# Repeating 1/sum by ScalarE and four transposes, with a new model of transfers and new leads in a list-scheduled Mamba and local-attention kernel

## The chip, the cores and the metric

The kernel runs on one core of a Trainium2 chip. The metric is the device time of one execution in microseconds; lower is better. A core has these engines, each with its own queue of instructions, worked off in order: PE (TensorE, matmuls; its weight loads are shown as PEld), DVE (VectorE), ACT (ScalarE), POOL (GpSimd) and SP (SyncE, which here issues nearly all transfers). Engines wait for each other by semaphores.

## The reference

The input is x, 4096 tokens of 256 features in float32. The output is x, plus a Mamba block, plus a two-layer local transformer, both applied to the same normalized x:

```
xn = layernorm(x)
out = x + mamba(xn) + local_transformer(xn)
```

The Mamba block projects 256 features to 2 x 512, convolves the first half over 4 tokens, and runs a recurrence over the tokens with 512 channels of 16 states each; the result is gated and projected back to 256. The transformer has two layers, each with local attention and an MLP of 682 gated hidden units. Attention has 8 heads of 64 features and windows of 128 tokens; a query sees the keys of its own window and of the window before:

```
attn = softmax(where(mask, -big, q @ k.T))   # per head and window
o = attn @ v                                 # 8 heads x 64 = 512 features
x = x + o @ wo
```

Softmax divides by the sum of the exponentials, one number for each query and head. The kernel multiplies the unnormalized `attn @ v` by 1/sum afterwards.

## The kernel before

**Tiles and stages.** The 4096 tokens are 16 stages of 256 tokens; each layer of the transformer goes through all 16, so there are 32 steps (l, s). A step projects two windows of 128 tokens (project), attends for both (attend), projects out (project_out) and runs the MLP (mlp). Beside them the Mamba block runs in 8 blocks of 512 tokens, each with 4 groups of 128 channels; one group of one block takes about one step. For each group, recur goes over the 16 states in 8 pairs: two loads of bc, copied to all partitions (L742 on, issued by SP at L451), a product u on POOL (L748), for each state a decay on ACT (L757), a scan on DVE (L762) and a product on DVE (L772), and transposes on PE that add up y (L784).

**Attention, around the change.** attend takes the heads in two groups of four. For each group PE multiplies queries and keys (L972), DVE masks and takes the largest (L987), ACT takes the exponential and its sum over the keys into den (L997), PE turns the probabilities (L1010), ACT copies them (L1014), and PE multiplies with V (L1026) into the bank po. There the features of a head lie over 64 partitions and the queries over columns. After both groups, den holds the sums with queries over partitions. DVE takes the reciprocal (L1043). To multiply, 1/sum has to lie like po: spread (L1049) has PE multiply one column of den, read 64 times as weights, by the identity, for each of 8 heads, in two halves of the array (part "columns"). ACT copies po into OT (L1055), DVE multiplies OT by the spread bank pd (L1056), and project_out reads OT (L1067).

**What sets the order.** Nothing in the code is in its final order. Each function records pieces of work by add (engine, estimated us, instructions, tiles read and written). A piece has a key: the time, in steps, at which its stage is due, minus its lead `soon`. Plan.order then simulates the engines: whenever one is free it takes, among the pieces whose inputs are ready and whose buffers are free, the one with the smallest key. Pieces with keys beyond the first open one plus AHEAD are not looked at. The instructions are emitted in the order of the simulated starts, and each engine on the chip then works off its own list in order. The estimates and the leads are therefore only an order: they are no waits. On PE a change of `part` (rows, columns, or the full array) is booked with SWITCH and avoided where another piece is nearly as urgent. `late` is the time from the end of an issue to the landing of a transfer. `holds` says which buffers a piece takes before it writes them. Buffers near the change: 5 PSUM banks, 2 OT tiles, 3 bc tiles, 3 u tiles, 2 PSUM tiles of decays.

**The planner's price of a transfer** is one line, in which kb is written out by hand at each call:

```
add("SP", 0.1, ..., late=2.4 + kb / 150.0, soon=soon)
```

The weights of each layer are loaded by load_qkv and load_rest; load_rest also has PE work out the shift of the MLP's bias (L487) and DVE scale w1 (L503).

Of the kernel before, what the change touches and what calls it, by code (L numbers as in the profile page):

```python
# [27 lines left out]
P = 128  # L28
# [3 lines left out]
TB = 512  # L32
# [10 lines left out]
AHEAD = 2.960000  # L43
# [93 lines left out]
class Plan:  # L137
# [4 lines left out]

    def __init__(self):
        self.works = []
        self.key = 0.0
# [35 lines left out]
    def order(self):  # L181
# [4 lines left out]
        part = ""  # L186
# [16 lines left out]
        while len(done) < len(self.works):  # L203
# [74 lines left out]
            w.start, w.end = start, start + w.us + self.TAIL[e] + w.late  # L278
# [35 lines left out]
def mamba_and_local_transformer(  # L314
# [38 lines left out]
    squares = buffer("sq", 2, [P, 512])  # L353
    turns = buffer("turn", 5, [P, HEADS, 2, DH // 2])
# [94 lines left out]
    def dma(kb, to, of, reads=(), writes=(), soon=0.0):  # L449

        add("SP", 0.1, lambda: nc.sync.dma_start(to(), of()), reads, writes, late=2.4 + kb / 150.0, soon=soon)  # L451

    def load_qkv(l):
        for s in range(3):
            cut = slice(s * INNER, (s + 1) * INNER)
            dma(
                512, lambda cut=cut: wqkv.ap[:, :, cut],
                lambda cut=cut: wqkv_d[l][:, cut].rearrange("(k p) n -> p k n", p=P), writes=[(wqkv, s)], soon=-0.25,
            )

    def load_rest(l):
        dma(512, lambda: wo.ap, lambda: wo_d[l].rearrange("(h p) n -> p h n", p=P), writes=[wo], soon=-0.09)
        for half in range(2):
            for m, n in ((0, WHOLE), (NM - 1, LAST)):
                to, of = w1_at(half, m), half * HID + m * MC
                dma(
                    n, lambda to=to, n=n: w1.ap[:, :, to : to + n],
                    lambda of=of, n=n: w1_d[l][:, of : of + n].rearrange("(k p) n -> p k n", p=P),
                    writes=[(w1, (half, m))], soon=-0.18,
                )  # L470
        whole = WHOLE
        dma(
            570, lambda: w2.ap[:, 0 : NM - 1, :],
            lambda: w2_d[l][0:whole, :].rearrange("(m p) n -> p m n", p=MC), writes=[(w2, 0)], soon=0.54,
        )
        dma(112, lambda: w2.ap[0 : HID - whole, NM - 1, :], lambda: w2_d[l][whole:HID, :], writes=[(w2, 1)], soon=-0.26)
# [28 lines left out]
        add("PE", 5.3, shift, [w1], [pb], soon=-0.73)  # L505
        add("DVE", 0.4, bias, [pb], [b1, b1x], soon=-0.28)
        add("DVE", 3.2, scale, [], [w1], port=True, soon=-0.24)
# [14 lines left out]
    def base_of(s):  # L522

        base = plan.value(rows_b)
        if s in sums:
            dma(256, lambda: base.ap, lambda: sums[s].ap, [sums[s]], [base], soon=-0.84)
            return base
        dma(256, lambda: base.ap, lambda: rows(x, s), writes=[base], soon=-0.12)
# [3 lines left out]
            ), [], [base], soon=-0.65,  # L532
# [3 lines left out]
    def finish(s, po, base):  # L536

        add("DVE", 0.6, lambda: nc.vector.tensor_tensor(base.ap, halves(po), base.ap, ALU.add), [po], [base], soon=-0.42)  # L538
        if s in sums:
            dma(256, lambda: rows(out, s), lambda: base.ap, [base], soon=0.37)  # L540
            return
        sums[s] = plan.fixed(dram.tile([P, NW, D], F32, tag=f"sum{s}", name=f"sum{s}"))
        dma(256, lambda: sums[s].ap, lambda: base.ap, [base], [sums[s]], soon=0.0)
# [4 lines left out]
    def shift_column(l, s):  # L548
        now = xts[l, s]
        if s == 0:  # L550
            add("POOL", 0.14, lambda: nc.gpsimd.memset(now.ap[:, 1, 0:1], 0.0), [], [(now, 0)], soon=0.49)
        else:
# [3 lines left out]
                [(old, 1)], [(now, 0)], soon=1.36,  # L556
            )

    def normalize(s):

        xb, mv, rstd, pt = (plan.value(b) for b in (rows_b, small["mv"], small["rstd"], banks))
        dma(256, lambda: xb.ap, lambda: rows(x, s), writes=[xb], soon=-0.18)
# [26 lines left out]
        add("DVE", 1.1, stats, [xb], [mv], soon=-1.39)  # L589
        add("ACT", 0.5, root, [mv], [rstd], soon=-0.35)  # L590
        add("DVE", 0.6, centre, [mv, rstd], [xb], port=True, soon=-0.91)
        now = xts[0, s] = plan.value(tokens)
        add("PE", 0.44, turn, [xb], [pt], holds=[now], soon=0.0)
        add("ACT", 0.48, lambda: nc.scalar.copy(now.ap[:, :, 1:], halves(pt)), [pt], [(now, 1)], soon=0.13)
        shift_column(0, s)
        dma(256, lambda: xn_d[s].ap, lambda: now.ap[:, :, 1:], [(now, 1)], [xn_d[s]], soon=-0.71)
# [3 lines left out]
    def reload(s):  # L600
        now = xts[1, s] = plan.value(tokens)
        dma(256, lambda: now.ap[:, :, 1:], lambda: x1_d[s].ap, [x1_d[s]], [(now, 1)], soon=-1.45)
# [6 lines left out]
    def in_half(i):  # L609
# [3 lines left out]
            lambda: in_wT[:, i * DI : (i + 1) * DI].rearrange("(k p) n -> p k n", p=P), writes=[w], soon=0.07,  # L613
# [3 lines left out]
    def in_proj(b, w, c, to):  # L617
# [9 lines left out]
        add("PE", 1.72, emit, [w, xms[b]], [pm], holds=[to], soon=0.09)  # L627
        return pm

    def front_load(b):  # L630
        xm = xms[b] = plan.value(xms_b)
        for i in range(PB):
            s = b * PB + i
            dma(
                256, lambda i=i: xm.ap[:, :, i * TS : (i + 1) * TS], lambda s=s: xn_d[s].ap, [xn_d[s]], [(xm, i)], soon=0.28
# [5 lines left out]
    def front_conv(b, c, w):  # L641
        xin, xc, tail = plan.value(rows_m), xcs[b], tails[b]
        edge = slice(c * (TAPS - 1), (c + 1) * (TAPS - 1))
        if b == 0:
            add("POOL", 0.14, lambda: nc.gpsimd.memset(xin.ap[:, 0 : TAPS - 1], 0.0), [], [(xin, 0)], soon=-0.34)
        else:
# [3 lines left out]
                [(old, c)], [(xin, 0)], soon=-0.31,  # L650
            )
        pm = in_proj(b, w, c, xin)
        add("ACT", 0.48, lambda: nc.scalar.copy(xin.ap[:, TAPS - 1 :], pm.ap), [pm], [(xin, 1)], soon=-0.44)
        if b < NB - 1:
            add(
                "POOL", 0.14, lambda: nc.gpsimd.tensor_copy(tail.ap[:, edge], xin.ap[:, TB:]), [(xin, 1)], [(tail, c)], soon=-0.19
            )
# [4 lines left out]
            ), [], [pm], soon=1.5,  # L662
# [8 lines left out]
        for j in range(TAPS - 1):  # L671
            add("DVE", 0.7, lambda j=j: tap(j), [xin, pm], [(xc, c) if j == TAPS - 2 else pm], soon=-0.95)

    def silu(v):
# [4 lines left out]
        add("ACT", 4.52, emit, [], [v], soon=-0.61)  # L679

    def front_dbl(b):
# [7 lines left out]
        add("PE", 3.43, emit, [xc], [px], holds=[xd], soon=-0.69)  # L689
        add("ACT", 0.48, lambda: nc.scalar.copy(xd.ap, px.ap[0:n]), [px], [xd], soon=-0.79)  # L690
        xds[b] = xd
        bc = bcs[b] = plan.fixed(dram.tile([2 * NS, TB], F32, tag=f"bc{b}", name=f"bc{b}"))
        dma(64, lambda: bc.ap, lambda: xd.ap[DTR:, :], [xd], [bc], soon=-0.28)

    def gate_conv(b, c, w):
# [4 lines left out]
        add("ACT", 0.48, lambda: nc.scalar.copy(sz.ap[:, c, :], pz.ap), [pz], [(sz, c)], soon=-1.39)  # L700

    def prepare(b, c):
# [7 lines left out]
            ), [xd], [pd], holds=[dt, e], soon=0.11,  # L710
# [3 lines left out]
        add("ACT", 0.59, lambda: nc.scalar.activation(e.ap[:, n], pd.ap, AF.Abs, bias=col("dt_b", c)), [pd], [e], soon=-0.35)  # L714
        add("ACT", 0.6, lambda: nc.scalar.activation(dt.ap, pd.ap, AF.Relu, bias=col("dt_b", c)), [pd], [dt], soon=1.17)
        add("ACT", 0.54, lambda: nc.scalar.activation(e.ap[:, n], e.ap[:, n], AF.Exp, scale=-1.0), [], [e], soon=-0.02)
        add(
            "DVE", 0.36, lambda: nc.vector.tensor_scalar(r.ap[:, n], e.ap[:, n], 1.0, -1.0, ALU.add, ALU.add),
            [e], [r], port=True, soon=0.7,
        )  # L720
        add("POOL", 1.22, lambda: nc.gpsimd.tensor_tensor(r.ap[:, n], e.ap[:, n], r.ap[:, n], ALU.subtract), [e], [r], soon=0.72)
        add("ACT", 0.6, lambda: nc.scalar.activation(e.ap[:, n], e.ap[:, n], AF.Ln, bias=one_t), [], [e], soon=-0.38)
        add("POOL", 1.22, lambda: nc.gpsimd.tensor_tensor(dt.ap, dt.ap, r.ap[:, n], ALU.add), [r], [dt], soon=1.1)
        add("POOL", 1.22, lambda: nc.gpsimd.tensor_tensor(dt.ap, dt.ap, e.ap[:, n], ALU.add), [e], [dt], soon=-0.41)
        add(
            "DVE", 0.61, lambda: nc.vector.tensor_tensor(dtx.ap, dt.ap, xc.ap[:, c, :], ALU.mult),
            [dt, (xc, c)], [dtx], port=True, soon=1.04,
# [3 lines left out]
    def recur(b, c, g):  # L731
# [6 lines left out]
        for s in range(2):  # L738
            w = plan.value(spreads)
            dma(  # L740
                256, lambda w=w: w.ap.rearrange("p n t -> p (n t)"),
                lambda s=s: bc.ap.rearrange("(s n) t -> s n t", s=2)[s, g * NG : (g + 1) * NG, :]  # L742
                .rearrange("n t -> (n t)").partition_broadcast(P), [bc], [w], soon=-0.15,
# [6 lines left out]
            ), [dtx, spread[0]], [u], soon=1.13,  # L750
        )
        for i in range(NG):
# [6 lines left out]
                ), [dt], [h], soon=0.32,  # L759
# [4 lines left out]
                ), [(u, i), (state, (c, n))], [h], soon=-0.6,  # L764
            )
            if b < NB - 1:
                add(
                    "ACT", 0.1, lambda h=h, n=n: nc.scalar.copy(state.ap[:, c, n : n + 1], h.ap[:, TB - 1 : TB]),  # L768
                    [h], [(state, (c, n))], alone=[h], soon=1.5,
# [4 lines left out]
                ), [h, spread[1]], [(u, i)], alone=[h], soon=-0.09,  # L774
# [4 lines left out]
        if n_sums == 1:  # L779
            add("POOL", 1.22, lambda: nc.gpsimd.tensor_tensor(u.ap[:, 0, :], u.ap[:, 0, :], u.ap[:, 1, :], ALU.add), [], [u], soon=-0.01)  # L780
# [13 lines left out]
        for i in range(n_sums):  # L794
            add("PE", 0.44, lambda i=i: collect(i), [(u, i)], [y], soon=0.31)

    def close(b, c):
# [3 lines left out]
        add("ACT", 0.48, lambda: nc.scalar.copy(ytv(), y.ap), [y], [yt], soon=0.43)  # L801

        def turn():
# [3 lines left out]
        add("PE", 0.44, turn, [yt], [py], soon=-0.05)  # L807
# [3 lines left out]
            ), [py], [(xc, c)], soon=1.5,  # L811
# [3 lines left out]
            [sz], [(xc, c)], soon=0.29,  # L815
        )

    def out_load():
# [3 lines left out]
            writes=[w], soon=0.29,  # L822
# [3 lines left out]
    def out_proj(b, i, w):  # L826
# [12 lines left out]
        add("PE", 3.44, emit, [w, xc, base], [po], soon=-0.75)  # L839
# [5 lines left out]
    def rotation(l, s):  # L845
        rot, trig = plan.value(rots), plan.value(trigs)
        dma(
            128, lambda: rot.ap, lambda: rot_d[s * TS : (s + 1) * TS].rearrange("(t p) s d -> p t s d", p=P),
            writes=[rot], soon=-0.22,
        )  # L850
        for i, scales in enumerate((qks, qkw)):
            for q in range(2):
# [6 lines left out]
                    ), [rot], [(trig, (i, q))], soon=-0.33,  # L859
# [3 lines left out]
    def project(l, s, t):  # L863
# [3 lines left out]
        def matmuls(q, holds):  # L867
# [10 lines left out]
            add("PE", 1.72, emit, [xb, (wqkv, q)], [pm], holds=holds, soon=-0.07)  # L878
# [4 lines left out]
        def norm(q, pm, sq):  # L883
            add("ACT", 0.48, lambda: nc.scalar.activation(sq.ap, pm.ap, AF.Square), [pm], [sq], alone=[pm], soon=-0.06)
# [3 lines left out]
                ), [sq], [(nrm, q)], soon=-0.52,  # L888
# [10 lines left out]
        def turned(parts, to):  # L899
            add("POOL", 1.22, lambda: nc.gpsimd.tensor_tensor(parts[0].ap, parts[0].ap, parts[1].ap, ALU.add), [parts[1]], [parts[0]], soon=-0.42)  # L900
# [9 lines left out]
            add("PE", 0.44, emit, [parts[0]], [pt], holds=[to], soon=-0.39)  # L910
# [456 lines left out]
```

## Time and profile before

| what | value |
|---|---|
| median of 3 runs | 1978.17 us (1977.82 to 1978.35) |
| the profiled execution's own time | 1979.39 us |
| its span in the profile | 1977.6 us |
| PE busy, instructions | 1917.6 us (97%), 13200 |
| DVE busy, instructions | 1742.4 us (88%), 3182 |
| ACT busy, instructions | 1490.5 us (75%), 3530 |
| POOL busy, instructions | 1411.3 us (71%), 1178 |
| mean clock granted to PE | 0.995 |
| DMA | 334.74 MB, mean 169 GB/s |

The span goes from the first to the last instruction of the core; the execution's own time is 1.8 us longer, which lies around the span. A float32 matmul has two records in the profile, a transpose one. Busy time is the time in which at least one record of an engine runs. A group is named by its line, its engine and what it writes and reads (out<-in); behind the bar stand its busy time, the mean of one record and the idle time of the engine just before it, with what ended that idle time. The chain that ended last is followed back from the last instruction.

### The profile page before, as it was taken

What the parts mean: (1) busy time and instruction counts of PE and PEld (TensorE: products, weight loads), DVE (VectorE), ACT (ScalarE), POOL (GpSimd) and SP (SyncE); (2) the same over time, 40 slices, a digit from 0 to 9 for tenths busy, and PEclk for the clock granted to TensorE, in tenths of its full rate; (3) what the DMA queues carried; (4) which work ended last, traced back from release to release, by engine and by line L of the source; (5) the groups of instructions that cost most, each with busy time, mean ns of one, the idle gap of its engine ahead of it and who ended that gap; (6) DMA issues with size and microseconds to landing.
All of it is one profiled execution on the core that took longest, in us unless ns stands there. A gap on an engine that the chain in (4) does not pass through costs nothing.

```text
span 1977.6 us, 37023 instructions
## 1 busy us (share of the span) xinstructions
PE 1917.6 (97%) x13200; PEld 1462.7 (74%) x13200; DVE 1742.4 (88%) x3182; ACT 1490.5 (75%) x3530; POOL 1411.3 (71%) x1178
## 2 busy tenths in 40 slices
PE   6999999999999999999999999999999999999997
PEld 3576777777777767777767777778777877777785
DVE  3789999999889999898997989889998898998895
ACT  2878877878777877777886787787887878777662
POOL 2668777777777777767785768877678767777773
PEclk9999999999999999999998999999999999999999
DMA  5445455644455445555465544455445654445453
GB/s 171 138 142 163 168 188 168 206 147 168 157 190 184 167 150 168 168 198 183 164 212 174 195 133 164 167 190 197 147 167 171 197 177 155 165 158 181 139 181 113
DMA packets 133928, 334.74 MB, mean 169 GB/s; under 512 B 13452, under 2 KB 57184, under 8 KB 133744
## 3 DMA queue, kind: packets, MB, share of 16 engines
q1 hardware_dynamic: 132752, 331.92, 50.7%
q8 instruction: 104, 1.70, 0.3%
q10 hardware_dynamic: 992, 0.46, 0.1%
q14 instruction: 80, 0.66, 0.1%
HBM read 315.03 MB, written 17.30 MB: 168 GB/s over the span
## 4 chain that ended last, share of the span: by engine, by line
PE 73%; DVE 12%; ACT 6%; DMA 4%; POOL 3%; issue 2%; SPq 0%; POOLq 0%; DVEq 0%; ACTq 0%
PE mm L873 12%; PE mm L1131 12%; PE y L784 7%; PE mm L1026 5%; PE mm L1067 5%; PE mm L972 5%; PE mm L623 5%; PE mm L1010 4%; PE mm L1213 4%; DVE da L762 3%; PE mm L1194 3%; DMA bc<-bc 2%; PE mm L905 2%; PE mm L1049 2%; DVE u L772 2%
## 5 line engine op out<-in xcount | busy, mean ns | idle before, releaser
L748 POOL TENSOR_TENSOR u<-dtx,bc 128x1024 f32<-128x1024 f32 x256 | 605.8, 2367 | 222.3 <-DMA bc<-bc 129.1
L762 DVE TENSOR_TENSOR_SCAN da<-da,state,u 128x512 f32<-128x512 f32 x448 | 562.2, 1278 | 60.7 <-POOL u L748 41.1
L757 ACT ACTIVATE da<-dt,negA 128x512 f32<-128x512 f32 x512 | 346.7, 693 | 95.6 <-DVE u L772 88.7
L873 PE MATMUL mm<-wqkv,xt 128*128 128x512 f32 x768 | 361.7, 604 | 1.3 <-DVE OT L1056 0.8
L772 DVE TENSOR_TENSOR u<-da,bc 128x512 f32<-128x512 f32 x512 | 339.1, 678 | 6.8 <-ACT state L768 2.2
L1131 PE MATMUL mm<-hn,w 128*128 128x256 f32 (+1 forms) x1408 | 329.4, 382 | 3.8 <-DVE mlp L1181 2.3
L1131 PEld LDWEIGHTS mm<-hn,w 128*128 128x128 f32 (+1 forms) x1408 | 259.2, 189 | 59.4 <-issue 15.9
L997 ACT ACTIVATE pr<-pr,top 128x256 f32<-128x256 f32 (+1 forms) x512 | 251.7, 494 | 32.6 <-DVE top L987 32.1
L873 PEld LDWEIGHTS mm<-wqkv,xt 128*128 128x128 f32 x768 | 138.9, 193 | 126.1 <-issue 113.4
L784 PE MATMUL y<-ident,u 128*128 128x128 f32 x1536 | 217.3, 276 | 13.6 <-POOL u L780 7.2
L987 DVE CUSTOM_DVE_ANT_0 pr<-mm,maskf,nrm 128x256 f32<-128x256 f32 (+1 forms) x512 | 213.3, 473 | 11.4 <-PE mm L972 10.9
L940 POOL TENSOR_TENSOR turn<-turn,trig 128x512 f32<-128x512 f32 x128 | 162.1, 1289 | 83.2 <-DVE turn L933 83.0
L784 PEld LDWEIGHTS y<-ident,u 128*128 128x128 f32 x1536 | 176.6, 141 | 52.9 <-issue 18.7
L780 POOL TENSOR_TENSOR u<-u 128x512 f32<-128x512 f32 x128 | 166.0, 1297 | 63.4 <-DVE u L772 55.4
L900 POOL TENSOR_TENSOR turn<-turn,turn 128x512 f32<-128x512 f32 x128 | 163.7, 1279 | 48.0 <-DVE turn L920 46.9
L768 ACT COPY state<-da 128x1 f32<-128x1 f32 x448 | 71.5, 162 | 110.0 <-DVE da L762 97.3
L1010 PEld LDWEIGHTS mm<-ident,pr 128*128 128x128 f32 x1008 | 114.8, 141 | 40.9 <-issue 14.9
L972 PEld LDWEIGHTS mm<-kT,qT 64*128 64x128 f32 x2016 | 121.3, 187 | 30.7 <-issue 13.0
L1014 ACT COPY prT<-mm 128x512 f32<-128x512 f32 (+1 forms) x256 | 138.1, 587 | 5.6 <-PE mm L1010 4.5
L972 PE MATMUL mm<-kT,qT 64*128 64x128 f32 x2016 | 139.7, 282 | 1.9 <-DVE top L987 1.1
L1010 PE MATMUL mm<-ident,pr 128*128 128x128 f32 x1008 | 133.3, 275 | 3.0 <-ACT prT L1014 2.0
L1026 PE MATMUL mm<-prT,v 128*64 128x128 f32 x2016 | 128.7, 277 | 1.5 <-DVE io L538 0.8
(128 smaller groups left out, 3498.2 us busy)
## 6 DMA issues: line engine op xcount, KB each, us to landing
bc<-bc SPq DMA_DIRECT2D x512, 512.0 KB, 4.0
io<-in_x SPq DMA_DIRECT2D x32, 256.0 KB, 4.4
mw<-in_in_wT SPq DMA_DIRECT2D x16, 512.0 KB, 3.8
rot<-in_rot SPq DMA_DIRECT2D x32, 128.0 KB, 4.1
xn<-xt SPq DMA_DIRECT2D x16, 256.0 KB, 4.1
xm<-xn SPq DMA_DIRECT2D x16, 256.0 KB, 4.7
x<-mid SPq DMA_DIRECT2D x16, 256.0 KB, 3.1
mw<-in_out_wT SPq DMA_DIRECT2D x8, 512.0 KB, 4.0
```

Of the source, the lines that this page charges most:

```text
L748: "POOL", 2.35, lambda: nc.gpsimd.tensor_tensor(u.ap, dtx.ap.unsqueeze(1).to_broadcast([P, NG, TB]), spread[0].ap, ALU.mult), [dtx, spread ...
L757: "ACT", 0.63, lambda h=h, n=n: nc.scalar.activation(h.ap, dt.ap, AF.Exp, scale=negA[:, c * NS + n : c * NS + n + 1]), [dt], [h], soon=0.32,
L762: "DVE", 1.18, lambda h=h, n=n, i=i: nc.vector.tensor_tensor_scan(h.ap, h.ap, u.ap[:, i, :], state.ap[:, c, n : n + 1] if b else 0.0, ALU. ...
L772: "DVE", 0.61, lambda h=h, i=i: nc.vector.tensor_tensor(u.ap[:, i, :], h.ap, spread[1].ap[:, i, :], ALU.mult), [h, spread[1]], [(u, i)], a ...
L784: nc.tensor.matmul(y.ap[:, t, :], lhsT=u.ap[:, i, t * P : (t + 1) * P], rhs=ident, is_transpose=True, start=g == 0 and i == 0 and t == 0, ...
L873: nc.tensor.matmul(pm.ap, lhsT=hT[k], rhs=wqkv.ap[:, k, q * INNER : (q + 1) * INNER], start=k == 0, stop=k == KC - 1,)
L972: nc.tensor.matmul(halves(scs[j])[:, i, a * WIN : (a + 1) * WIN], lhsT=qT.ap[half, 2 * g + i, :], rhs=kk.ap[half, 2 * g + i, :], start=n == 0,
L987: nc.vector.tensor_tensor_reduce(out=prs[j].ap[:, i, keys], in0=halves(scs[j])[:, i, keys], in1=mask[:, keys], scale=nrm.ap[:, h : h + 1], ...
L997: nc.scalar.activation(prs[j].ap[:, i, keys], prs[j].ap[:, i, keys], AF.Exp, bias=top.ap[:, h : h + 1], scale=-1.0, accum_out=den.ap[:, h ...
L1010: nc.tensor.transpose(ppv()[:, j, a, :], prs[j].ap[:, i, a * WIN : (a + 1) * WIN], ident)
L1026: nc.tensor.matmul(hpair(po.ap)[j * DH : (j + 1) * DH, hp, :], lhsT=vv.ap[:, h * DH : (h + 1) * DH], rhs=prT.ap[:, j, a, :], start=a == first,
L1131: nc.tensor.matmul(halves(pm)[0:r, i, :], lhsT=w1.ap[:, k, c0 : c0 + r], rhs=hn.ap[:, k, :], start=k == 0, stop=k == KC - 1,)
```

## The change

**The spread of 1/sum.** The 8 half-width products are replaced. ACT writes den, each sum 64 times, into a new SBUF tile wide (128x512, one buffer), and PE turns it in four full transposes:

```
-        pd = plan.value(banks)
+        wide, pd = plan.value(wides), plan.value(banks)
         add("DVE", 0.08, reciprocal(den.ap, den.ap), ...)
+        add("ACT", 0.48, lambda: nc.scalar.copy(
+                wide.ap.rearrange("p (h d) -> p h d", d=DH), den.ap.unsqueeze(2).to_broadcast([P, HEADS, DH])
+            ), [den], [wide], soon=1.5)
         def spread():
             for hp in range(HP):
-                for j in range(2):
-                    h = 2 * hp + j
-                    nc.tensor.matmul(
-                        hpair(pd.ap)[j * DH : (j + 1) * DH, hp, :], lhsT=den.ap[:, h : h + 1].to_broadcast([P, DH]),
-                        rhs=ident, start=True, stop=True,
-                    )
-        add("PE", 0.54, spread, [den], [pd], part="columns", soon=-0.44)
+                nc.tensor.transpose(hpair(pd.ap)[:, hp, :], wide.ap[:, hp * P : (hp + 1) * P], ident)
+        add("PE", 0.44, spread, [wide], [pd], soon=-0.3)
```

**The planner's transfers.** A transfer now takes at least TRANSFER from its issue, and after that shares one rate with those before it. An issue is booked with 0.32 us. Some sizes written by hand change: bc loads from 256 to 512, rot from 128 to 256, the two parts of w2 from 570 and 112 to 640 and 42.

```
+    TRANSFER, RATE = 2.2, 300.0
...
-            w.start, w.end = start, start + w.us + self.TAIL[e] + w.late
+            w.start, w.end = start, start + w.us + self.TAIL[e]
+            if e == "SP":
+                w.end = moved = max(start + self.TRANSFER, moved) + w.late / self.RATE
...
-        add("SP", 0.1, ..., late=2.4 + kb / 150.0, soon=soon)
+        add("SP", 0.32, ..., late=kb, soon=soon)
```

**Other prices and leads.** The shift of load_rest is booked with 8.3 instead of 5.3 us, its scaling with 4.6 instead of 3.2. AHEAD goes from 2.96 to 2.36. Nearly every `soon` has a new value between -1.5 and 1.5; a larger one makes a piece due earlier. Those that the prediction names, and some of the largest moves:

```
 piece                         line          before  after
 u<-dtx,bc          POOL       L748           1.13   -0.5
 decay              ACT        L757           0.32    1.32
 scan               DVE        L762          -0.6    -1.0
 pair sum           POOL       L780          -0.01    1.5
 xc update in close DVE        L809           1.5    -0.88
 down, layer 0      PE         L1194         -1.24    0.63
 down_rows, layer 1 PE         L1213         -1.5     0.83
 up                 PE         L1131         -0.2    -1.12
 wqkv loads         SP         L451          -0.25    0.74
 wo load            SP         L451          -0.09    1.05
 bc loads           SP         L451          -0.15   -0.19
 sum stores         SP         L451           0.0    -1.15
```

What is computed, the buffers other than wide, the transfers and their bytes stay the same.

## The prediction

> **What bounds the kernel now.** I read the page's engine totals first, then busy time by stretch of the span, then PE's timeline, then the waits. The totals and the chain:
>
> ```profile
> PE 1917.6 (97%) x13200; PEld 1462.7 (74%) x13200; DVE 1742.4 (88%) x3182; ACT 1490.5 (75%) x3530; POOL 1411.3 (71%) x1178
> ...
> PE 73%; DVE 12%; ACT 6%; DMA 4%; POOL 3%; issue 2%; SPq 0%; POOLq 0%; DVEq 0%; ACTq 0%
> ```
>
> PE is nearly always busy and makes up 73% of the chain that ended last. Cut into head, middle and tail (columns: length, then PE, PEld, DVE, ACT, POOL busy):
>
> ```profile
> 0.00:120.00 120.00, 95.75 (x532) 61.37 (x533) 71.33 (x164) 72.27 (x170) 58.03 (x79) 0.99 0.50 158
> 120.00:1900.00 1780.00, 1759.04 (x12249) 1347.96 (x12248) 1621.36 (x2943) 1384.96 (x3301) 1317.15 (x1078) 1.00 0.52 171
> 1900.00:1977.60 77.60, 62.76 (x423) 53.40 (x421) 49.71 (x76) 33.27 (x61) 36.11 (x23) 0.96 0.43 141
> ```
>
> In 1780 us of middle, PE idles 21 us; the head has 24 us of idle and the tail 15. So the middle is bound by PE's stream, and what leaves that stream should leave the time. A busy share alone doesn't prove this, since ends of matmuls are modelled. So I go by distances from start to start in PE's timeline (start, length, operation, records):
>
> ```profile
> 1003.60 0.60 PE L784 MATMUL y<-ident,u 128*128 128x128 f32 x4
> 1004.03 0.60 PE L905 MATMUL mm<-ident,turn 128*128 128x128 f32 x4
> 1004.47 5.35 PE L1131 MATMUL mm<-hn,w 128*128 128x256 f32 x24
> ...
> 1011.05 1.09 PE L1026 MATMUL mm<-prT,v 128*64 128x128 f32 x16
> 1011.98 1.04 PE L1049 MATMUL mm<-ident,den 128*64 128x128 f32 x16
> 1012.95 5.42 PE L873 MATMUL mm<-wqkv,xt 128*128 128x512 f32 x12
> ...
> 1031.19 1.14 PE L1026 MATMUL mm<-prT,v 128*64 128x128 f32 x16
> 1032.27 1.12 PE L708 MATMUL mm<-xd,dtw 16*128 16x512 f32 x2
> ```
>
> Groups follow each other without a hole. Four transposes (L784, L905) take a step of 0.43 to 0.44 us. The spread of 1/sum (L1049) takes 0.97 here; over the 56 spreads that directly follow the last product with V (L1026) the median step is 1.02. L1026 takes 0.93 when another half-width group follows and 1.08 when a full-width one does: leaving the half-width form costs about 0.10 to 0.15, now paid at the end of the spread.
>
> **The change, part by part.** *The spread.* Each of 64 windows loses 8 half-width matmuls (16 records) and gets 4 transposes (4 records). Its PE step falls from 1.02 to 0.44; the change of form, about 0.10, stays, now behind L1026. That is 1.02 − 0.44 − 0.10 = 0.48 us, times 64 = **31 us**. Were the change of form to vanish too, 0.58 × 64 = 37 us; the group rows below give 69.7 − 256 × 0.151 = 31 us (0.151 is 77.4 us over 512 transposes). I take 31, on which two countings agree.
>
> ```profile
> L1049 PE MATMUL mm<-ident,den 128*64 128x128 f32 x1024 | 69.7, 273 | 0.0
> L905 PE MATMUL mm<-ident,turn 128*128 128x128 f32 x512 | 77.4, 274 | 0.5 <-DVE top L987 0.3
> L1110 ACT ACTIVATE sq<-hn 128x512 f32<-128x512 f32 x32 | 20.2, 630 | 5.6 <-DVE hn L1108 5.5
> L748 POOL TENSOR_TENSOR u<-dtx,bc 128x1024 f32<-128x1024 f32 x256 | 605.8, 2367 | 222.3 <-DMA bc<-bc 129.1
> ```
>
> A rule speaks against this part. The Trainium skill, "TensorEngine Tiling (Array Packing)", When to Use Tiling, advises two column tiles where the stationary operand is 64 or fewer columns wide, as it is in the old spread, for up to twice the speed. By that alone eight paired half-width products cost what four full ones do, the step would not change, and the sum would stay at about 1979. The same page, Key Properties, has a change of tiling mode drain the array, which is the 0.10 us I see.
>
> *ScalarE's copy.* It adds 64 writes of 128x512, SBUF to SBUF. The nearest row is L1110, the same size between the same memories: 0.63 us, so 40 us more on ACT, from 75% to about 79% of the new span. The copy of the unscaled output (L1055, 0.59) stays. The path reciprocal, copy, transposes, product (L1056) gets longer by 0.63 plus one hand-over, less 0.48. What covers it: from the end of the reciprocal to the first matmul of the spread lie 12.7 us in the median, and only two of the 64 have under 1 us. Consumers of OT (L1067, L873) waited for it under 4 us in total. So I cost it at nothing. Without that cover it costs at most 64 × 0.63 = 40 us. The copy also waits for the reciprocal at the head of ACT's queue; behind it stand the decays (L757) and the copies of probabilities (L1014), which PE needs. One new tile, wide, has one buffer and is freed by its four transposes.
>
> *The transfers in the planner.* No transfer is added or enlarged: 740 issues on SP before and after. Only the planner's belief changes, and with it the order.
>
> ```profile
> bc<-bc SPq DMA_DIRECT2D x512, 512.0 KB, 4.0
> io<-in_x SPq DMA_DIRECT2D x32, 256.0 KB, 4.4
> ```
>
> Before, a bc load was booked as 256 KB: 0.1 + 2.4 + 256/150 = 4.2 us, each for itself. Now it is 512 KB: 2.2 + 512/300 = 3.9 alone, 3.9 + 1.7 = 5.6 for the second of a pair. The trace has 4.0 in the median, 1.6 to 7.7 at the ends; it has 0.32 us per issue where the old plan had 0.1. Both new figures are nearer. Gain, if bc loads come better: PE's idle before L784, 13.6 us, is all that this chain costs PE directly; POOL's 129 us (L748) are hidden. The loss, if SP's order gets worse, is unknown; SP is one queue in order, and it stands at bc issues for L772 and L748 to free buffers (624 and 403 us):
>
> ```profile
> SPq L451 <- DVE u L772: 623.8, 209, 9.0
> SPq L451 <- POOL u L748: 402.9, 187, 8.8
> ```
>
> A late store or load of tokens behind such an issue is late with it.
>
> *The leads.* Some hundred priorities move, by up to 2.4 steps of the plan (32 steps in 1978 us, some 60 us each), and the horizon shrinks from 2.96 to 2.36 steps. They change whom a queue serves first, not the work: u on POOL (L748) falls by 1.63, its decay on ACT (L757) rises by 1.0, down (L1194, L1213) rises by 1.87 and 2.33. On SP a layer's weights move about one step earlier (wqkv by 0.99, wo by 1.14) and the sums' stores 1.15 later, past bc loads; each is one issue of 0.32 us. The plan's wrong price of shift (5.3; L487 takes 18.2 us in two, so 9.1) becomes 8.3. Bounds: PE's whole idle, 60 us, as a gain; as a loss, the rival below on the other side. I take 2 us of gain, from the one wait of 10.2 us that L487 has for w at 11.5 us; its price and that of the loads are what was mended. That is a choice, near nothing because PE idles only 1.2% of the middle.
>
> **The sum.** The profiled execution took 1979.4 us, 1.8 around its span of 1977.6. Minus 31 gives 1948.4; minus 2 gives 1946.4. The runs' median, 1978.2, is 1.2 below the profiled execution, so **1945 us**, 1.7% faster. With 64 × 0.63 on ACT, DVE at 1742 is 90% of the new span: nearer to a bound, not yet one.
>
> **The rivals.**
> - *The new order also fills holes.* For it: prices of transfers, shift and spread (0.54 planned, 1.02 in the trace; now 0.44 planned and 0.44 in the trace) come nearer to the chip, and head and tail hold 39 us of idle. Against: the middle has little to give. A third to a half of 60 us: 1916 to 1936, say 1926.
> - *ACT takes a part back.* Every second copy lies on the path, 32 × 0.63 = 20 us: 1957 to 1974, say 1965. For it: ACT is in order and PE waits for its copies. Against: the 12.7 us of cover.
> - *The removed PE time was hidden anyway*, or DVE takes over at once: 1974 to 1982. Against it: 21 us of idle in 1780.
> - *Slower: the scan's chain becomes the bound.* Place: u on POOL, whose lead falls by 1.63 steps, then the scan (L762), then L772 on DVE. DVE idles 159 us in the middle now, and may idle 159 − 31 = 128 in the forecast. If each of the 32 passes (8 blocks of 4 channel groups) uncovers one load and its product, 4.0 + 2.37 = 6.4 us, that is 204 us. It decides from 5.1 us a pass (163 us): at 5.4 the time is 1978 + 14 = 1992, at 6.4 it is 2023. For it: DVE already waits 41 us for L748. Against: three buffers of u and of bc.
>
> **Chances and range.** Forecast (1936 to 1957) 0.45; holes filled 0.25; part taken back 0.15; hidden 0.07; slower 0.08. Runs tell about 0.2%, 4 us, from no change: faster 0.85, same 0.07, slower 0.08. The range 1918 to 1972 reaches over the first three and leaves out the last two and the edges. The PE bounds (31 to 37) and half of PE's idle lie inside.
>
> **What would show it.** PE should have 13200 − 1024 + 256 = 12432 records, ACT 3594, DVE and POOL as many as before. The transposes of wide: 256 records, 0.44 us per four; PE busy near 1886. The copy: 0.59 to 0.64 us, 64 times. Middle: PE idle still 1 to 2%. If DVE's or POOL's wait at L762 and L748 grows and PE idles over 3% of the middle, the fourth rival is right. If PE idle in head and tail falls by 10 us or more, the first is. The prediction is wrong if the copy is over 1 us, if four transposes of wide take over 0.6, or if PE's idle moves by over 25 us either way.

## The result and the profile after

The changed kernel takes 1957.0 us in the median of 4 runs (1952.3 to 1961.7); before takes 1978.3 on the same chip. The ratio is 0.9891, 95% interval [0.9866, 0.9916]: 1.1% faster, 21 us, where 33 were forecast. The profiled execution took 1958.1 us, its span is 1956.3. Totals and chain of after, and its head, middle and tail (columns as before):

```profile
PE 1896.4 (97%) x12432; PEld 1434.2 (73%) x12432; DVE 1725.8 (88%) x3182; ACT 1526.3 (78%) x3594; POOL 1406.9 (72%) x1178
...
PE 73%; DVE 11%; ACT 8%; POOL 3%; issue 2%; DMA 2%; POOLq 0%; DVEq 0%; ACTq 0%
```

```profile
0.00:120.00 120.00, 103.89 (x605) 66.85 (x607) 82.86 (x188) 83.27 (x205) 67.33 (x87) 0.97 0.52 168
120.00:1900.00 1780.00, 1748.91 (x11623) 1330.85 (x11619) 1610.58 (x2952) 1425.43 (x3364) 1317.13 (x1078) 0.99 0.52 173
1900.00:1956.30 56.30, 43.63 (x211) 36.52 (x210) 32.34 (x44) 17.63 (x27) 22.40 (x16) 0.94 0.37 122
```

The counts are those forecast: 12432 records on PE, 3594 instructions on ACT. PE's busy time fell by 21.2 us, to 1896.4 where 1886 was forecast, and the span by 21.3. PE idles 60 us, as before, but elsewhere: 16 instead of 24 in the head, 31 instead of 21 in the middle, 13 instead of 15 in the tail. The spread in PE's timeline, and the two new groups (instructions, busy, mean):

```profile
1002.74 2.02 PE L1032 MATMUL mm<-prT,v 128*64 128x128 f32 x32
1004.69 0.66 PE L790 MATMUL y<-ident,u 128*128 128x128 f32 x4
1005.19 0.60 PE L1058 MATMUL mm<-ident,wide 128*128 128x128 f32 x4
1005.72 2.06 PE L978 MATMUL mm<-kT,qT 64*128 64x128 f32 x32
...
1026.45 0.60 PE L1058 MATMUL mm<-ident,wide 128*128 128x128 f32 x4
1026.89 0.60 PE L911 MATMUL mm<-ident,turn 128*128 128x128 f32 x4
```

```profile
L1058 PE MATMUL mm<-ident,wide 128*128 128x128 f32 x256 | 40.9, 282 | 1.4 <-DVE top L993 0.7 <-ACT prT L1020 0.4 <-DVE xc L815 0.2
L1051 ACT COPY wide<-den 128x512 f32<-128x512 f32 x64 | 39.2, 613 | 0.6 <-DVE den L1049 0.2
```

Four transposes take a step of 0.44 before another full-width group and 0.53 before a half-height one (1005.19 to 1005.72); over all 64 spreads the median step is 0.49, where the old spread's is 1.02. The copy takes 0.61 us, and ACT stands idle before it for 0.6 us in all.

### The profile page after: what moved, and what is told of

It reads as the page before. It is cut to its first block, busy times and chain, and to the rows that moved or that the text cites. A ratio compares the mean times of both kernels' runs of the same rounds, so it can differ in the third digit from the quotient of the medians.

```text
span 1956.3 us, 35501 instructions
## 1 busy us (share of the span) xinstructions
PE 1896.4 (97%) x12432; PEld 1434.2 (73%) x12432; DVE 1725.8 (88%) x3182; ACT 1526.3 (78%) x3594; POOL 1406.9 (72%) x1178
## 4 chain that ended last, share of the span: by engine, by line
PE 73%; DVE 11%; ACT 8%; POOL 3%; issue 2%; DMA 2%; POOLq 0%; DVEq 0%; ACTq 0%
PE mm L879 13%; PE mm L1137 12%; PE y L790 6%; PE mm L978 5%; PE mm L1073 5%; PE mm L1032 5%; PE mm L629 4%; PE mm L1016 4%; PE mm L1219 4%; DVE da L768 4%; PE mm L1200 3%; PE mm L840 3%; PE mm L911 2%; POOL u L754 2%; DVE u L778 2%
## 5 line engine op out<-in xcount | busy, mean ns | idle before, releaser
L768 DVE TENSOR_TENSOR_SCAN da<-da,state,u 128x512 f32<-128x512 f32 x448 | 562.9, 1278 | 61.7 <-POOL u L754 33.1
L1137 PE MATMUL mm<-hn,w 128*128 128x256 f32 (+1 forms) x1408 | 339.9, 385 | 4.5 <-DVE top L993 1.9
L1137 PEld LDWEIGHTS mm<-hn,w 128*128 128x128 f32 (+1 forms) x1408 | 259.2, 191 | 66.0 <-issue 16.4
L790 PEld LDWEIGHTS y<-ident,u 128*128 128x128 f32 x1536 | 179.2, 141 | 57.1 <-issue 23.1
L978 PEld LDWEIGHTS mm<-kT,qT 64*128 64x128 f32 x2016 | 120.8, 188 | 26.9 <-issue 17.6
L978 PE MATMUL mm<-kT,qT 64*128 64x128 f32 x2016 | 139.0, 282 | 0.0
```

Source lines behind the costliest of these rows:

```text
L768: "DVE", 1.18, lambda h=h, n=n, i=i: nc.vector.tensor_tensor_scan(h.ap, h.ap, u.ap[:, i, :], state.ap[:, c, n : n + 1] if b else 0.0, ALU. ...
L790: nc.tensor.matmul(y.ap[:, t, :], lhsT=u.ap[:, i, t * P : (t + 1) * P], rhs=ident, is_transpose=True, start=g == 0 and i == 0 and t == 0, ...
L978: nc.tensor.matmul(halves(scs[j])[:, i, a * WIN : (a + 1) * WIN], lhsT=qT.ap[half, 2 * g + i, :], rhs=kk.ap[half, 2 * g + i, :], start=n == 0,
L1137: nc.tensor.matmul(halves(pm)[0:r, i, :], lhsT=w1.ap[:, k, c0 : c0 + r], rhs=hn.ap[:, k, :], start=k == 0, stop=k == KC - 1,)
```

## The experiments

**The theories.** P: PE's stream alone sets the time; then the exchange of the spread takes its 31 us off, and 10 us were lost elsewhere. Either the new order lost them (theory A of runs 1 and 2), or ACT's copy took them back (theory B of runs 1 and 2, theory A of run 3). Against P stands S: a us off PE is worth less than a us, because PE then waits more often for lists that didn't get faster. From run 7 on each expectation says what its letters mean. Runs 1, 2, 7 and 8 ran on one chip, the repeat of after and runs 3 to 5 on another, runs 6 and 9 to 11 on a third. On the first, 20 runs of before spread from 1971.9 to 1984.7 us, so I compare ratios to before on the same chip.

**1. The exchange in the order of before.** The copy is put into ACT's list ahead of each spread, the spread becomes the four transposes, and nothing else moves (shortened):

```
+        copies = sorted((max(r.end + 0.1, m.start - 2.5), r.then) for r, m in self.moved)
         for w in works:
+            while copies and copies[0][0] <= w.start: copies.pop(0)[1]()
             w.emit()
```

Where two windows' spreads stand next to each other (seen once in the trace of before), the first reads the second's sums; the work is the same.

> The order of before is kept on every engine; only the spread is exchanged: the copy of 1/sum is put into ACT's list at most 2.5 us (planned time) ahead of its four transposes. Theory A (the exchange is worth its full 31 us on PE, and the new order with its holes and clock drops gave about 10 back): 1978 - 31 = 1947 us, PE busy 1886 or less. Theory B (the exchange itself is worth only 21 us, because the copy delays ACT and PE waits for it; the new order is neutral): 1957 us, with PE idle or ACT waits up by 10 us.

Measured: 1969.6 us, ratio 0.9949 [0.9931, 0.9967], 10 us. Theory A's 1947 is far off, and so is theory B's 1957.

```profile
PE 1896.2 (96%) x12432; PEld 1433.4 (73%) x12432; DVE 1738.6 (88%) x3182; ACT 1520.2 (77%) x3594; POOL 1410.4 (72%) x1178
```

PE's busy time fell by 21 us, but its idle time rose from 60 to 71. A part of this is the place that the copy was given here: PE waits for it (us in total, times, longest).

```profile
PE mm L1059 <- ACT wide L1053: 2.8, 2, 2.3
```

That is 2.8 us in two waits of the middle, 2.3 of them in one. So run 1 is not the bare worth of PE's time in the old order; the old order without the copy was not run.

**2. The order of after with the old spread.**

```
-        add("ACT", 0.48, <copy of den into wide>, [den], [wide], soon=1.5)
+        add("ACT", 0.48, lambda: None, [den], [wide], soon=1.5)
-                nc.tensor.transpose(...)
+                for j in range(2): nc.tensor.matmul(..., lhsT=den.ap[:, h : h + 1].to_broadcast([P, DH]), rhs=ident)
```

> The order of after is kept on every engine; the spread is again 8 half-width products read straight from the sums, and the copy is left out of ACT's list. Theory A (new order costs about 10 us): after + 31 = 1988 us. Theory B (new order neutral, exchange worth 21): 1978 us.

Measured: 1977.5, ratio 0.9989 [0.9972, 1.0006]. The new order by itself can't be told from the old one; A falls. Against after (0.9891) the exchange gives 0.9902, or 19 us, in the new order; the two intervals together leave some 7 us on either side.

```profile
PE 1924.7 (98%) x13200; PEld 1460.3 (74%) x13200; DVE 1721.9 (87%) x3182; ACT 1497.9 (76%) x3530; POOL 1407.0 (71%) x1178
```

**After once more**, on the chip of the three that follow:

> The changed kernel as it is, for comparison on this chip with the three that follow and with the exchange in the old order. Expected 21 us below before, as measured first.

Measured: 1955.4, ratio 0.9891 [0.9861, 0.9922].

```profile
PE 1894.1 (97%) x12432; PEld 1431.6 (73%) x12432; DVE 1720.9 (88%) x3182; ACT 1525.8 (78%) x3594; POOL 1405.9 (72%) x1178
```

Between run 2 (span 1973.2) and this one (1951.2) PE's busy time differs by 30.6 us: in the new order the exchange takes the forecast 31 off PE's work. Idle grows from 48.5 to 57.1, so 22.0 are left in the span. Both lost the same 13.7 us to the granted clock (its distance from 1, added up over the span), so the clock is not what took the rest. Some of PE's waits in the middle, run 2 first, then after:

```profile
PE mm L714 <- ACT OT L1062: 2.5, 2, 1.4
PE y L790 <- DVE u L778: 0.3, 1, 0.3
```

```profile
PE mm L714 <- ACT OT L1061: 4.2, 4, 1.6
PE y L790 <- DVE u L778: 1.9, 2, 1.2
```

The order is the same, so I paired PE's records (12176 without the spread) and added up how the difference of their starts grows (gained: the kernel with the exchange lets PE start earlier) and shrinks (lost: PE waits there where it didn't). A loss that is made up again counts in both columns; after is this second execution:

```
stretch, us      before to run 1           run 2 to after
                 gained  lost   net        gained  lost   net
120-540             7.3   9.5  -2.2          11.5   4.7   6.8
540-1040           10.9   9.6   1.3          13.5   6.5   7.0
1100-1500           7.9   3.5   4.4           8.2   6.3   1.9
1500-1890           6.7   3.4   3.3           7.9   3.5   4.4
```

The stretches left out (head, 1040 to 1100, tail) net some 3 us in the old order and 2 in the new one. A single stretch is uncertain by some 4 us: between the two executions of after, 1100 to 1500 differs by 4.3. In the old order the whole first layer (120 to 1040 us) gives nothing, and run 6 below, in the same order, agrees with 0.8 us net. Losses are spread over many small waits: in run 1, over the whole span and counting steps of 0.05 us or more, 7.3 us at 26 places before PE adds up y (the recurrence's products), 4.7 at 18 before the MLP's first product, 4.1 at 9 before turned queries and keys. Lines that carry the middle's two layers, before and then run 1:

```profile
120.00:1040.00 920.00, 905.85 (x6284) 685.80 (x6284) 857.69 (x1565) 725.18 (x1754) 686.85 (x568) 1.00 0.52 173
1100.00:1890.00 790.00, 784.72 (x5567) 608.20 (x5564) 707.24 (x1285) 615.42 (x1449) 587.56 (x478) 1.00 0.50 168
```

```profile
120.00:1040.00 920.00, 894.73 (x5901) 671.25 (x5899) 857.52 (x1564) 740.15 (x1782) 685.38 (x567) 1.00 0.53 173
1100.00:1890.00 790.00, 783.61 (x5259) 601.18 (x5258) 711.63 (x1293) 631.77 (x1485) 593.08 (x483) 1.00 0.52 170
```

In the first 920 us of the middle DVE does the same work in both (857.7 and 857.5 us, 1565 and 1564 instructions), and PE only idles more (14 and 25 us). In the second stretch DVE gets through 8 instructions more.

**3. Is it ACT's copy?** The order of after, without the copy:

```
+    nc.gpsimd.memset(wides.tiles[0], 0.01)
-            "ACT", 0.48, <copy of den into wide>, [den], [wide], soon=1.5
+            "ACT", 0.48, lambda: None, [den], [wide], soon=1.5
```

> Order of after on every engine. ACT's copy of 1/sum is left out: the four transposes turn a constant tile that is filled once, so the division by the sums is missing from the result. ACT has 39 us less to do, the path from reciprocal to product has no ACT in it. Theory P (PE's stream alone sets the time, the 10 missing us are the clock's and chance): within 4 us of after. Theory A (ACT's copy gave 10 us back): 8 to 15 us below after, PE idle down by as much.

Measured: 1955.3, ratio 0.9886 [0.9861, 0.9912], as after. ACT's busy time is 29 us lower and the time stays, so theory A's 8 to 15 us fall: in this order the copy costs nothing that shows.

```profile
PE 1895.1 (97%) x12432; PEld 1432.1 (73%) x12432; DVE 1723.2 (88%) x3182; ACT 1496.4 (77%) x3530; POOL 1406.5 (72%) x1179
```

**4. What a us of PE is worth.** The transposes twice, in the order of after:

```
+                for _ in range(2):
                     nc.tensor.transpose(hpair(pd.ap)[:, hp, :], wide.ap[:, hp * P : (hp + 1) * P], ident)
```

> Order of after on every engine, each of the four transposes of the spread is made twice, 28 us more for PE (64 x 0.44). Theory P (PE's stream alone): after + 28. Theory S (PE shares the limit with DVE and ACT, whose lists it waits for now and then; a us of PE is worth about two thirds): after + 15 to 20, with PE idle down by 8 to 13.

Measured: 1973.1, ratio 0.9976 [0.9959, 0.9994]: after + 17.

```profile
PE 1918.3 (97%) x12688; PEld 1460.9 (74%) x12688; DVE 1721.3 (87%) x3182; ACT 1526.3 (77%) x3594; POOL 1406.7 (71%) x1178
```

At the spreads the paired records are 27.5 us later in all, so PE did get its 28 us. Of them 17 reach the time, about 0.6; the exchange itself gives 19 for 31, the same. With some 7 us of uncertainty on each, 0.4 to 0.85 is open, and 1 is not: theory P falls. Theory S has the time right, but PE's idle went from 57.1 down to 51.5 only, 6 us and not 8 to 13.

**5. and 6. Is it DVE's load?** DVE's last product on half of the columns, in the order of after (5) and in run 1 (6):

```
-        tensor_tensor(OT.ap, OT.ap, hpair(pd.ap), ALU.mult)
+        tensor_tensor(OT.ap[:, 0:2], OT.ap[:, 0:2], hpair(pd.ap)[:, 0:2], ALU.mult)
```

> Order of after on every engine, DVE multiplies only half of the columns of OT by 1/sum, so half of the heads stay undivided: some 0.3 x 64 = 19 us less for DVE and nothing else. Theory P: within 4 us of after. Theory S: a part of these 19 us, 5 to 12, leaves the time, as holes of PE that DVE's lateness makes.

> As the exchange in the old order, and DVE multiplies only half of the columns of OT by 1/sum (half of the heads stay undivided), some 0.3 x 64 = 19 us less for DVE. Theory D (in the first layer of the old order DVE, 93% busy there, sets the pace as much as PE, and this is why the exchange brought nothing in the first 1000 us): 8 to 12 us below the exchange in the old order, nearly all of it in the first layer. Rival L (the lists' waits for each other set the pace, not one engine's load): within 4 us of the exchange in the old order.

Measured: (5) 1961.7, ratio 0.9918 [0.989, 0.9946], no gain on after; (6) 1969.1, ratio 0.9941 [0.992, 0.9961], no gain on run 1 (0.9949).

```profile
PE 1896.0 (97%) x12432; PEld 1432.3 (73%) x12432; DVE 1708.1 (87%) x3182; ACT 1525.2 (78%) x3594; POOL 1405.5 (72%) x1178
PE 1895.3 (96%) x12432; PEld 1435.0 (73%) x12432; DVE 1727.8 (88%) x3182; ACT 1518.9 (77%) x3594; POOL 1410.2 (72%) x1178
```

DVE's busy time is 13 us lower in (5) than in after and 11 lower in (6) than in run 1, where 19 were expected, and PE idles 72 us in (6), as in run 1 (71). The 8 to 12 us of theory D, which stood on DVE's 93% in the first layer, are not seen. But the edit was only some 60% of what was planned, half of it lies in the second layer, and the times resolve about 5 us, so a smaller part played by DVE's load isn't excluded. Waits from list to list (rival L) fit; which chain of them it is in the first layer was not singled out.

**7. to 11. What the order is worth.** Two plans with the leads of before: the new spread with everything else of before (7), and with the new prices too (8). The copy has the lead of after (1.5) in both, the spread itself that of after (-0.3) in (7) and of before (-0.44) in (8).

> Prices of transfers, leads and horizon of before; the new spread is planned as in after, so the whole order is made anew with leads that were not chosen for it. Theory A: the exchange gives 31, an order whose leads don't fit takes some back: 1947 to 1962 us. Theory B: 1957 us or slower. If it is slower than 1965, leads matter more than the exchange.

> The new spread and the new prices, with the leads and the horizon of before (the copy's lead is that of after). Against e3 this shows what the prices of transfers do without their leads. Theory A (order is a matter of how well leads fit): within 10 us of e3, either side, some 1950 to 1970 us. The rival that the new prices alone make the order better: 5 us or more below e3, and POOL's wait for bc loads below the 145 us of after.

Three with the leads of after: old prices (9), AHEAD 2.96 (10), and six pairs of states added on POOL (11), the one try at a kernel faster than after:

```
(9)  -  TRANSFER, RATE = 2.2, 300.0      and the old prices of transfers, shift and scaling
(10) -AHEAD = 2.360000                   +AHEAD = 2.960000
(11) -PAIRED = (1, 3, 5, 7)              +PAIRED = (1, 2, 3, 5, 6, 7)
```

> The changed kernel, new leads and horizon, with the prices of before (each transfer for itself, 0.1 us an issue, shift 5.3, scaling 3.2). If the new prices make the order good: 10 us or more above after, 1966 or higher. If the leads do, whatever the prices: within 5 us of after. From the pair with old leads (1996 with old prices, 1976 with new ones) I expect some 20 us above after, 1976.

> The changed kernel with AHEAD 2.96 instead of 2.36. If a longer horizon is harmless (only few pieces are ready that early): within 4 us of after. If leads fit only with their own horizon: 8 us or more above after.

> The changed kernel with six of eight pairs of states added on POOL before PE turns them, instead of four; the leads are those of after, the order is made anew. PE loses 64 x 0.44 = 28 us, POOL gains 64 x 1.28 = 82 us (72% to 77%). By the worth of a us of PE seen so far (0.63): 18 us below after, 1938. Rival (an order that its leads weren't chosen for costs more than it saves, as in the spread replanned with old leads): 5 to 25 us above after.

Measured:

```
                                     us      ratio to before
(7)  new spread, rest of before    1996.3   1.0087 [1.0059, 1.0115]
(8)  new spread, prices; old leads 1976.2   0.9978 [0.9962, 0.9993]
(9)  after, old prices             2019.3   1.0192 [1.0166, 1.0218]
(10) after, old horizon            1997.2   1.0076 [1.0046, 1.0106]
(11) after, six pairs              2011.3   1.0145 [1.0121, 1.017]
     after                         1955.4   0.9891 [0.9861, 0.9922]
```

By the ratios, every plan that mixes leads with prices, a horizon or work that they weren't put together with is 17 to 60 us above after, although PE has the same instructions to run in (7) to (10), and 256 transposes (28 us) fewer in (11):

```profile
PE 1897.6 (94%) x12176; PEld 1412.4 (70%) x12176; DVE 1743.8 (87%) x3182; ACT 1521.8 (76%) x3594; POOL 1483.7 (74%) x1242
```

In (11) PE idles 114 us (2011.2 − 1897.6) instead of 57, and its busy time isn't even lower than that of after (1894.1), at a mean granted clock of 0.984 instead of 0.993. Of the expectations, (7) lies above theory A's range, and beyond the 1965 from which leads were to matter more than the exchange. In (8) theory A falls, as it is 20 us below (7); its rival has the time right but not its sign, as POOL waits 169 us for bc loads and not under 145. (9) is 60 us above after where I expected 20; (10) went the way of "leads fit only with their own horizon", and (11) that of its rival, by more than its 25 us. (9) and after differ by 60 us through prices alone, which are in no instruction; (7) and (8) differ by 20 through prices and the spread's own lead. Prices and leads can't be valued apart.

## Why the prediction was right, and where it was too large

Direction and range held (1918 to 1972, wide enough for two of the rivals as well); 1945 was 12 us too low, and 1957.0 lies on the upper edge of the forecast's own band (1936 to 1957).

- *PE's work*: right. The two countings gave 31 us; run 2 and after differ by 30.6 in PE's busy time. The sign "PE busy near 1886" was missed all the same: run 2, the new order with the old spread, has 1924.7, 7 us more than before, of which 3.4 go with the clock (13.7 us lost to it, before 10.2). And in the old order busy time fell by only 21.4 us (run 1): a transpose's record is 0.27 us long at a step of 0.11, so a wait shorter than the difference counts as busy.
- *The rule that spoke against it.* The Trainium skill, "TensorEngine Tiling (Array Packing)", When to Use Tiling, advises two column tiles for a stationary operand of 64 columns. Record for record this trace agrees: a half-width one takes a step of 0.06 us (16 in 0.93), a full-width one 0.11 (4 in 0.44). What decides is the number of records: a float32 product has two, a transpose one, so 16 half-width records gave way to 4 full ones.
- *"What leaves that stream should leave the time"*: the term that was mis-sized. I let 31 us of PE count as 31 us of time, because PE idled only 21 us in the middle. Runs 4 and 2 show 0.6 of it in the new order; run 1 shows a third in the old one, with some 3 us of direct waiting for the copy in it, so that there the rival "hidden anyway" is nearer than its 0.07. An engine that is busy 98.8% can still be paced by others: each exchange lets it start 0.5 us earlier, and some records on it stands before something that didn't move. That it stands more is shown (idle 48.5 to 57.1 us); which lists pace it is not. 31 × 0.6 = 19, with 2 for the order, would have given 1957.
- *ACT's copy at nothing*: right in the new order (run 3). The time came out at the lower edge of the rival "ACT takes a part back", but not by its mechanism.
- *Leads and prices, 2 us of gain*: the net was right. With the old spread the new order is 0.11% below before, some 2 us, with an interval from 0.28% below to 0.06% above, so it isn't told from nothing. But my reason was wrong. I took the order to be nearly harmless, as PE idles so little; runs 7 to 11 show that another order is easily 17 to 60 us worse. That two orders, each with leads of its own, came out equally good was luck as far as my reasoning goes.
- *The sign for filled holes*: it came, and misled. Idle in head and tail fell from 39 to 29 us, the 10 that were to speak for the first rival, but the middle's rose by as much, and no time was gained.
- *Loads of bc*: POOL's wait for them rose from 129 to 145 us and cost nothing visible.

```profile
L754 POOL TENSOR_TENSOR u<-dtx,bc 128x1024 f32<-128x1024 f32 x256 | 605.5, 2365 | 210.4 <-DMA bc<-bc 145.1
L768 DVE TENSOR_TENSOR_SCAN da<-da,state,u 128x512 f32<-128x512 f32 x448 | 562.9, 1278 | 61.7 <-POOL u L754 33.1
```

- *Slower by the scan's chain*: not seen. DVE's wait for u fell from 41.1 to 33.1 us.

## What to carry to other kernels

A high busy share bounds what an engine can still idle, not what a us taken off it is worth: measure that slope by doubling a small piece of its work in the same order, before counting a saving at full price. Judge an edit under a list scheduler with the order held fixed, and apart from that with an order and leads of its own. Planned anew with leads made for something else, even less work on PE came out slower here (runs 7, 9, 10 and 11 against before).

## What else the runs showed of the hardware

A hole on PE costs more than its length. In two executions of after, PE's timeline agrees to within a us up to about 1130 us. Then the second falls behind, and the first comes 2.7 us earlier to the product that needs the copy of v (its group before starts at 1284.73, the second's at 1287.46). There it waits 2.62 us, and the second doesn't wait at all. First execution, timeline and stretches (after PEld, DVE, ACT and POOL comes the granted clock), then the second's stretches:

```profile
1284.73 1.16 PE L978 MATMUL mm<-kT,qT 64*128 64x128 f32 x16
1288.51 3.58 PE L629 MATMUL mm<-xm,mw 128*128 128x512 f32 x4 [2.62 <-ACT v L952]
1291.88 2.04 PE L1137 MATMUL mm<-hn,w 128*128 128x256 f32 x8
```

```profile
1280.00:1290.00 10.00, 7.11 (x38) 4.28 (x38) 10.00 (x9) 4.72 (x13) 7.37 (x8) 0.94 0.27 104
1290.00:1300.00 10.00, 10.00 (x54) 7.08 (x53) 8.87 (x21) 7.86 (x20) 9.05 (x9) 0.89 0.29 95
```

```profile
1280.00:1290.00 10.00, 9.76 (x53) 6.12 (x53) 9.79 (x13) 7.32 (x17) 10.00 (x9) 1.00 0.17 63
1290.00:1300.00 10.00, 10.00 (x60) 7.59 (x59) 10.00 (x27) 9.24 (x25) 9.89 (x10) 1.00 0.47 158
```

In the first execution the granted clock is 0.94 and 0.89 there, and the four records of L629 take a step of 3.37 us instead of 1.82. From the start of L978 to that of L1137 it takes 7.15 us, the second 2.92: a hole of 2.62 us cost 4.2, so PE's lead was waited away and 1.5 us more lost. The traces' own record of the clock has 1.00 or 0.50 only, in stretches that are multiples of 3.41 us; here it is 0.50 from 1288.76 to 1292.17, after 3.41 us in which PE was busy for 0.79. The Trainium skill, "TensorE: Matmul & The Clock Gate", Part 1, tells of a gate that halves the clock after an idle window of about 3.4 us. The halving and the 3.4 us agree, but the window need not be idle throughout: a hole of 2.62 us was enough, at 1402 us even one of 1.43, while one of 1.93 at 519 us cost no clock. Added up over the span, the clock cost 10.2 us in the profile of before, 17.1 in the first of after and 13.7 in the second; so some of the distance between executions of one kernel (1952.3 to 1961.7) seems to come from where such holes happen to fall. That was read from the traces, and not tried by itself.

One DVE product of 128x512 in SBUF (dtx) took 1.08 us in the mean before and 0.74 after, the same instruction in another place of the lists; DVE's busy time in it fell by 11 us. What it ran beside was not looked into, so the cause is open.
